# A Restormer-style block on one core: which bands put a chunk of the convolution on TensorE, where the first image's attention keeps its sums, and a new order

## The chip, the cores and the metric

The kernel runs on one core of a Trainium2 chip. The metric is the device time of one execution in microseconds; a kernel is run several times and the median is compared.

## The reference

The input x is 16 images of 128 channels and 96 × 96 pixels, all in float32. For each image the block computes, in this order:

```python
xn = layernorm(x, over channels)                  # norm 1
q, k, v = xn @ wq.T, xn @ wk.T, xn @ wv.T         # 8 heads of 16 channels
q, k = l2norm over the pixels of q, k
attn = softmax(q @ k.T / sqrt(16))                # 16 x 16 per head, a sum over all 9216 pixels
x = x + (attn @ v) @ wp.T
xn = layernorm(x, over channels)                  # norm 2
h1 = conv1x1(xn, w_in)                            # 128 -> 512 channels
h2 = depthwise_conv3x3(h1, w_dw)
x = x + conv1x1(gelu(h2), w_out)                  # 512 -> 128 channels
```

The attention is over channels, so an image needs its whole norm 1 before the attention, and the attention before its norm 2.

## The kernel before

Channels lie on the 128 partitions and pixels along the free dimension. An image is cut into 8 **bands** of 12 rows (1152 pixels) and 24 **units** of 4 rows (384 pixels); 16 images make 128 bands, numbered g = 0 to 127. The 512 hidden channels are 4 **chunks** of 128.

**Norms** (`norm`, lines 475 to 632). Norm 1 is called a, norm 2 is called b. Four tiles of 128 pixels make a batch q, 18 in an image. TensorE transposes them so that pixels lie on partitions (`forth`, L533), DVE takes the statistics (`stats`, L539) and the variance (L546), GpSimd raises it to the power of −1/2 (`power`, L550), DVE makes the shift (`shift`, L554), and ScalarE writes the normalized tiles zT (`scaled`, L573; for the first image, which uses h banks for its transposes, DVE does half of them, L563). For norm 1 TensorE then adds the tiles' products with themselves into one 128 × 129 sum in PSUM (`gram`, L583). It transposes them back (`back`, L609), and ScalarE puts them into the padded image xn (`place`, L613 and L615). Norm 2 starts from x plus the attention's result (`x2`: `mix`, L491, and either `residual` on DVE, L497, or `mixed` on ScalarE with a DMA that adds x, L500 and L503).

**Attention** (`attention`, lines 634 to 759) works on the gram alone. It is a chain of small steps that alternate between TensorE, DVE, GpSimd and ScalarE. Its first step (L660) copies the gram to SBUF; the later ones use other columns of the gram's own PSUM bank for their results. The planner has one such bank, `g`.

**Feed forward.** A chunk of a band is made in one of two ways. In a DVE job (`conv_job`), TensorE makes the hidden rows (`hidden`, L783), ScalarE copies them to SBUF (`kept`, L788) and makes three of the nine products (`product`, L799), two of which are added by accumulating DMAs that GpSimd issues (`add_products`, L807); DVE adds the six other taps (`tap`, L803), and ScalarE applies the gelu (`gelu`, L811). In the very last job there are no such DMAs: DVE adds all eight taps, and the gelu goes unit by unit. Or, for chunk 3 only (`PE_CHUNK`), TensorE does the 1 × 1 and the 3 × 3 convolution as nine matmuls per unit with weights made beforehand (`by_matmuls`, L853), and ScalarE applies the gelu (L859). `by_pe` (L898) says for which bands. At the end `ffn_out` multiplies the four chunks with w_out per unit (L876), DVE adds the result to x (L883), and SyncE issues the store (L887). The order of the four products is

```python
order = sorted(range(NCH), key=lambda n: (n != PE_CHUNK, n))
```

which is chunk 3 first, then 0, 1, 2.

**The order of the work** is made by a planner (`Plan`, lines 46 to 196). Each step is given an engine, a time that it is expected to take, what it reads and writes, and a place: a number of jobs, to which the table `AT` adds an offset by the kind of step. The planner runs the steps through a small event simulation: when an engine is free, it takes the step with the lowest place of those whose inputs are there and for which a buffer is free. The order that comes out is the order in which each engine executes; semaphores keep the dependencies on the chip. The planner also counts the buffers: 4 PSUM banks `h` (shared by the products of mix, hidden, conv and out, by the first image's transposes and by the weights' transposes), 2 banks `tr`, 1 bank `g`, 3 buffers zT, 9 buffers h3, 4 buffers pr, 2 and 5 buffers x1 and xb for bands of x. A TensorE matmul in float32 shows as two records in the profile.

Of the kernel before, what the change touches and what calls it, by code (L numbers as in the profile page):

```python
# [18 lines left out]
BR = 12  # L19
# [2 lines left out]
PE_OF = 7  # L22
TINY = 1e-20
DMA_TAPS = (1, 2)
QT = 4
H_BANKS = 4
X1_BUFS, XB_BUFS, PR_BUFS, H3_BUFS, ZT_BUFS = 2, 5, 4, 9, 3
IN_TURN = ("tr", "h3", "pr", "xb", "x1")
AT = dict(
    weights=0.9, zeros=6.55, load_a=-14.05, forth_a=-8.8, stats_a=-11.5, variance_a=-13.4, power_a=3.35,  # L30
    shift_a=-4.85, scaled_a=-0.8, gram=-2.9, back_a=-19.8, place_a=-18.9, attention=-9.75, mix=-10.05,
    residual=-13.2, mixed=-4.5, add_x=4.65, forth_b=-6.15, stats_b=1.25, variance_b=-4, power_b=-19,
    shift_b=-16.6, scaled_b=0.85, back_b=-14.75, place_b=-1.75, halo=1.55, hidden=-0, kept=-5.25,
    product=-4.6, products=2.35, add_last=-9.55, tap=6, add_first=25.15, gelu=-2.6, conv=1.9,
    conv_gelu=-2.9, out=2.85, add=5.05, store=1.6,
)
STEP = dict(hidden=0.1, products=0.5, tap=0.166, conv=1.6, conv_tap=0.03, out=0.8, out_part=0.05)
SLACK = 300
NORM1_END = 6.0
EARLY = 5  # L40
WAIT = dict(POOL=350, SP=1300, ACT=1300)
T_ADD, T_MOVE = 3100, 1800


class Plan:
# [44 lines left out]
    def order(self):  # L90
# [38 lines left out]
        def dispatch(engine, time):  # L129
            queue = queues[engine]  # L130
            while queue:
                item = heapq.heappop(queue)
                k = item[1]
                lacks = room(k)
                if lacks is None:
                    break
                waiting.setdefault(lacks, []).append(k)
            else:
                return
            o = ops[k]  # L140
            starts[k] = time
            idle[engine] = False
            for t in o[5]:
                self.slot[t] = free[t[0]].pop(0)
                if t[0] in IN_TURN:
                    turn[t[0]].pop()
                    wake(t[0], time)
            ns, result, own = o[1], o[6], o[7]
            if o[8]:
                self.dma = max(time + ns + WAIT[engine], self.dma) + o[8]  # L150
                result = own = self.dma + result - time
            elif engine == "POOL":
                rest = self.two - time
                ns, result = (ns, result) if rest <= 0 else (rest + 705, rest + result)
                own = result
            if o[9]:
                self.two = time + ns + 35
            push(time + own, "own", k)
            push(time + ns, "idle", k)
            push(time + result, "done", k)  # L160
# [39 lines left out]
def tile_restormer_block(  # L200
# [32 lines left out]
    NTOK = H * W  # L233
    HP, WP = H + 2, W + 1
    D = C // HEADS
    assert PE_CHUNK == NCH - 1 and BR * W >= 8 * P and QT % 2 == 0 and NU * TPU % QT == 0 and C == P and UT % P == 0 and H % BR == 0 and NCH == 4

    xv = x.rearrange("b c h w -> b c (h w)")
    ov = out.rearrange("b c h w -> b c (h w)")
# [16 lines left out]
    make_block_diagonal(nc, blocks, D)  # L256
    ones = const.tile([P, 1], F32, name="ones")
    nc.gpsimd.memset(ones, 1.0)
    mhalf = const.tile([P, QT], F32, name="mhalf")
    nc.gpsimd.memset(mhalf, -0.5)  # L260

    def column(v, name):
# [212 lines left out]
    def norm(i, second, place_of):  # L475
# [38 lines left out]
                xb = [xtok(b * UPB + k) for k in range(UPB)]  # L514
                add(at("add_x", s), add_x, [], xb)

        def pixels(s, q):

            d = {}
            tiles = range(q * QT, (q + 1) * QT)  # L520
            early = i == 0 and (not second or q < EARLY)
            key_ = "h" if early else "tr"
            by_dve = QT // 2 if early else 0

            def forth():
                if early:
                    d["pT"] = bank((name, q)).rearrange("p (t c) -> p t c", c=P)
                else:
                    d["pT"] = p_tr.tile([P, QT, P], F32, tag="tr", name=f"pT_{name}_{q}")
                for t in tiles:  # L530
                    b, j = divmod(t, TPB)
                    xt = (xbs if x_key(i, b, second) == "xb" else x1s)[i, b]
                    nc.tensor.transpose(d["pT"][:, t - tiles[0], :], xt[:, j * P : (j + 1) * P], ident)  # L533

            def stats(j):

                if j == 0:
                    d["st"] = small.tile([P, QT // 2, 6], F32, tag="st", name=f"st_{name}_{q}")
                nc.vector.bn_stats(  # L539
                    d["st"][:, j, :], d["pT"][:, 2 * j : 2 * j + 2, :].rearrange("p t c -> p c t")  # L540
                )

            def variance():
                d["mv"] = d["st"].rearrange("p j (t v) -> p (j t) v", v=3)
                ve = d["ve"] = small.tile([P, QT], F32, tag="ve", name=f"ve_{name}_{q}")
                nc.vector.tensor_scalar(ve, d["mv"][:, :, 2], 1.0 / C, EPS, ALU.mult, ALU.add)  # L546

            def power():
                rstd = d["rstd"] = small.tile([P, QT], F32, tag="rstd", name=f"rstd_{name}_{q}")
                nc.gpsimd.tensor_tensor(rstd, d["ve"], mhalf, ALU.pow)  # L550

            def shift():
                nb = d["nb"] = small.tile([P, QT], F32, tag="nb", name=f"nb_{name}_{q}")
                nc.vector.scalar_tensor_tensor(nb, d["mv"][:, :, 1], -1.0, d["rstd"], ALU.mult, ALU.mult)  # L554
                if by_dve:
                    take_zT()

            def take_zT():
                zTs[q] = zT_bufs[plan.slot["zT", (name, q)]]

            def also_scaled():
                for j in range(by_dve):
                    nc.vector.tensor_scalar(  # L563
                        zTs[q][:, j, :P], d["pT"][:, j, :], d["mv"][:, j, 1:2], d["rstd"][:, j : j + 1],
                        ALU.subtract, ALU.mult,
                    )

            def scaled():
                if not by_dve:
                    take_zT()  # L570
                zT = zTs[q]
                for j in range(by_dve, QT):
                    nc.scalar.activation(  # L573
                        zT[:, j, :P], d["pT"][:, j, :], AF.Identity,
                        bias=d["nb"][:, j : j + 1], scale=d["rstd"][:, j : j + 1],
                    )

            def gram():
                if q == 0:
                    grams[i] = p_g.tile([P, 4 * P], F32, tag="g", name=f"g_{i}")  # L580
                for t in tiles:
                    zt = zTs[q][:, t - tiles[0], :]
                    nc.tensor.matmul(  # L583
                        grams[i][:, : P + 1], lhsT=zt[:, :P], rhs=zt, start=(t == 0), stop=(t == NU * TPU - 1)
                    )

            tr, bt, zt = (key_, (name, q)), ("batch", (name, q)), ("zT", (name, q))
            units = {t // TPU: None for t in tiles}
            pe(110 * QT, at("forth" + ab, s), forth, [xtok(u) for u in units], [tr])
            for j in range(QT // 2):  # L590
                dve(341, at("stats" + ab, s), lambda j=j: stats(j), [tr], [bt])
            dve(80, at("variance" + ab, s), variance, [], [bt])
            op("POOL", 848, at("power" + ab, s), power, [], [bt], 881 + SLACK)
            dve(80, at("shift" + ab, s), shift, [], [bt, (*zt, 2)] if by_dve else [bt])
            if by_dve:
                dve(by_dve * 240, at("scaled" + ab, s), also_scaled, [tr, bt], [(*zt, 0)])
            act((QT - by_dve) * 343, at("scaled" + ab, s), scaled, [tr, bt], [(*zt, 1)])
            if not second:
                pe(QT * 220, at("gram", s), gram, [(*zt, 0), (*zt, 1), ("w", "ones")], [("g", i)])

        def channels(s, u):

# [22 lines left out]
            for u in range(NU):  # L625
                x2(place_of(u * TPU), u)
        u = 0
        for q in range(NU * TPU // QT):
            pixels(place_of(q * QT), q)
            while u < NU and (u + 1) * TPU <= (q + 1) * QT:  # L630
                channels(place_of(u * TPU), u)
                u += 1

    def attention(s, i):
# [2 lines left out]
        places_of = dict(srow="ma", kq="ma", em="ma", y="ma", gs="mb", e="mb", a="mb", mT="mb")  # L637
        columns = dict(ps_s=128, ps_u=256, ps_r=0, ps_n=128, ps_kq=256, ps_qk=384, ps_y=0, ps_m=128, ps_d=256)
        v = {}

        def sb(shape, tag, pool=att):
            v[tag] = pool.tile(shape, F32, tag=places_of.get(tag, tag), name=f"{tag}_{i}")
# [2 lines left out]
        def ps(shape, tag):  # L645

            c = columns[tag]
            v[tag] = grams[i][: shape[0], c : c + shape[1]]
            return v[tag]

        def step(engine, ns, also=()):
            def add(f):
                op(engine, ns, s, f, [("w", "qk")], [("g", i), ("m", i), *also], ns + 200 + SLACK)
            return add

        wide = [("x1", ("attention", i))]

        @step("DVE", 210)
        def _():
            nc.vector.tensor_copy(sb([P, P + 1], "gs"), grams[i][:, : P + 1])  # L660
            v["gsb"], v["s"] = v["gs"][:, :P], v["gs"][:, P:]
# [43 lines left out]
        def _():  # L705
            nc.vector.tensor_scalar(sb([P, 2], "n2"), v["ps_n"], 1e-24, None, ALU.max)

        @step("POOL", 848)
        def _():
            nc.gpsimd.tensor_tensor(sb([P, 2], "rn"), v["n2"], mhalf[:, :2], ALU.pow)  # L710

# [184 lines left out]
            move(at("store", p), lambda: store(0, UPB), [("xb", (i, b), k) for k in range(UPB)], [], T_MOVE)  # L896

    def by_pe(g):  # L898
        return g % PE_OF in PE_BANDS

    NG = B * NB
    jobs, first = [], []
# [56 lines left out]
```

## Time and profile before

| | |
|---|---|
| median of 8 runs | 4418.47 us (4414.09 to 4421.56) |
| profiled execution, its own time | 4422.32 us |
| its span | 4420.6 us |
| TensorE (PE) busy | 4309.6 us |
| VectorE (DVE) busy | 4272.2 us |
| ScalarE (ACT) busy | 4060.2 us |
| GpSimd (POOL) busy | 1881.5 us |
| taps on DVE, L803 | 2636 of 1408 ns, 3655.3 us |
| matmuls of the conv, L853 | 3942 records of 486 ns |
| matmuls of the output, L876 | 3072 records of 492 ns |

In the lines of the profile, PE is TensorE and PEld its loading of weights, DVE is VectorE, ACT is ScalarE, POOL is GpSimd and SP is SyncE. A timeline line gives the start and the length in microseconds, the engine, the source line, the operation, what is written and read (`h<-h,dw,h`), the shape and the count of merged instructions; the brackets give the idle time of the engine before it and what ended that. A line of waits gives who waited for whom, the sum in microseconds, the number of times and the longest. A line of a stretch gives the stretch, its length, then for each engine the busy time and the number of instructions, the granted TensorE clock, the share of the DMA engines and GB/s. The time of a matmul is modelled, so records overlap and the mean of one is longer than the distance from one to the next.

### The profile page before, as it was taken

How to read it: one execution, taken by the hardware profiler on the slowest of the kernel's cores; microseconds unless marked ns; L12 is line 12 of the kernel's file. 1: busy time of each engine (PE TensorE's matmuls, PEld its weight loads, DVE VectorE, ACT ScalarE, POOL GpSimd, SP SyncE). 2: the span in 40 equal slices, each digit the busy share in tenths (PEclk: the TensorE clock that was granted, in tenths of full speed). 3: DMA queues.
4: the chain of work that ended last, by engine and by line, in shares of the span. 5: the costliest groups of instructions: out<-in, count | busy, mean ns of one | idle time of the engine just before them, and what ended most of it. 6: DMA issues, size and time to landing. Idle time of an engine off the chain costs nothing. (4 is left out here: it accounts for less than half of the span.)

```text
span 4420.6 us, 53360 instructions
## 1 busy us (share of the span) xinstructions
PE 4309.6 (97%) x17782; PEld 2752.1 (62%) x17782; DVE 4272.2 (97%) x5681; ACT 4060.2 (92%) x7071; POOL 1881.5 (43%) x1620
## 2 busy tenths in 40 slices
PE   7999999999999999999999999999999999999997
PEld 6656666666666666666666666666666666666554
DVE  5999999999999999999999999999999999999998
ACT  4999999999999999999999999999999999989885
POOL 3444444344444444444444444444445444444331
PEclk9999999999999999999999999999999999999998
DMA  2778788787888878788887887878888888878886
GB/s 78 161 162 174 169 174 179 166 182 161 182 172 168 183 163 178 168 172 179 168 176 167 180 174 162 182 167 178 173 170 179 168 178 170 169 169 162 171 169 134
DMA packets 183635, 744.52 MB, mean 168 GB/s; under 512 B 21312, under 2 KB 22720, under 8 KB 183360
## 3 DMA queue, kind: packets, MB, share of 16 engines
q0 software_dynamic: 143856, 589.30, 70.5%
q1 hardware_dynamic: 37152, 151.01, 9.3%
q8 instruction: 140, 2.29, 0.2%
q10 hardware_dynamic: 2352, 0.81, 0.1%
q14 instruction: 135, 1.11, 0.1%
HBM read 148.85 MB, written 75.50 MB: 51 GB/s over the span
## 5 line engine op out<-in xcount | busy, mean ns | idle before, releaser
L803 DVE SCALAR_TENSOR_TENSOR h<-h,dw,h 128x1152 f32<-128x1152 f32 x2636 | 3655.3, 1408 | 5.8 <-ACT h L799 1.5
L853 PE MATMUL h<-xn,comp 128*128 128x384 f32 x3942 | 1421.1, 486 | 8.6 <-ACT x L500 5.0
L799 ACT ACTIVATE pr<-h,dw 128x1152 f32<-128x1152 f32 x876 | 1131.9, 1302 | 26.5 <-DMA pr<-pr 25.8
L876 PE MATMUL h<-h,woutT 128*128 128x384 f32 x3072 | 1115.4, 492 | 41.7 <-ACT h L788 17.6
L783 PE MATMUL h<-xn,winT 128*128 128x384 f32 (+1 forms) x2634 | 1034.2, 500 | 6.1 <-ACT h L859 2.4
L853 PEld LDWEIGHTS h<-xn,comp 128*128 128x128 f32 x3942 | 718.8, 189 | 465.3 <-issue 16.1
L876 PEld LDWEIGHTS h<-h,woutT 128*128 128x128 f32 x3072 | 562.2, 191 | 400.9 <-ACT h L788 28.3
L807 POOL DMA_DIRECT2D h<-pr x438 | 406.5, 928 | 846.5 <-issue 139.4
L788 ACT COPY h<-h 128x384 f32<-128x384 f32 (+1 forms) x1317 | 654.9, 532 | 93.7 <-PE h L783 70.6
L807 POOL DMA_DIRECT2D pr<-pr x438 | 403.2, 921 | 747.8 <-ACT pr L799 590.1
L550 POOL TENSOR_TENSOR rstd_b<-ve_b,mhalf 128x4 f32<-128x4 f32 x288 | 521.6, 1812 | 384.9 <-DVE ve_b L546 358.7
L550 POOL TENSOR_TENSOR rstd_a<-ve_a,mhalf 128x4 f32<-128x4 f32 x288 | 509.9, 1775 | 390.9 <-DVE ve_a L546 378.5
L783 PEld LDWEIGHTS h<-xn,winT 128*128 128x128 f32 x2634 | 474.6, 190 | 305.2 <-issue 35.1
L811 ACT ACTIVATE h<-h 128x1152 f32<-128x1152 f32 x441 | 529.3, 1201 | 70.4 <-DMA h<-pr 67.5
L799 ACT ACTIVATE h<-h,dw 128x1152 f32<-128x1152 f32 x439 | 569.8, 1298 | 5.0 <-PE h L876 1.2
L573 ACT ACTIVATE zT<-pT_b,nb_b,rstd_b 128x128 f32<-128x128 f32 x1132 | 438.4, 509 | 14.6 <-DVE nb_b L554 13.2
L573 ACT ACTIVATE zT<-pT_a,nb_a,rstd_a 128x128 f32<-128x128 f32 x1080 | 417.4, 508 | 20.5 <-DVE nb_a L554 17.5
L583 PEld LDWEIGHTS g<-zT 128*128 128x128 f32 x2304 | 292.1, 191 | 40.1 <-issue 2.1
L583 PE MATMUL g<-zT 128*128 128x129 f32 x2304 | 305.6, 275 | 0.2 <-DVE zT L563 0.2
L491 PE MATMUL h<-xn,mwT 128*128 128x384 f32 x768 | 286.0, 489 | 3.0 <-ACT h L788 1.4
L613 ACT ACTIVATE xn<-pB_b,b 128x384 f32<-128x384 f32 x384 | 243.3, 634 | 22.8 <-PE pB_b L609 21.7
L539 DVE BATCH_NORM_STATS2 st_b<-pT_b 128x6 f32<-128x256 f32 x566 | 237.6, 422 | 5.6 <-PE pT_b L533 5.4
(111 smaller groups left out, 3246.8 us busy)
## 6 DMA issues: line engine op xcount, KB each, us to landing
pr<-pr POOLq DMA_DIRECT2D x438, 576.0 KB, 5.4
h<-pr POOLq DMA_DIRECT2D x438, 576.0 KB, 6.2
x<-in_x_dram SPq DMA_DIRECT2D x128, 576.0 KB, 5.5
out_dram<-x SPq DMA_DIRECT2D x127, 576.0 KB, 3.7
x<-in_x_dram POOLq DMA_DIRECT2D x123, 576.0 KB, 7.0
out_dram<-x SPq DMA_DIRECT2D x3, 192.0 KB, 1.8
weights<-in_L_conv_w_in_dram ACTq DMA_DIRECT2D x1, 256.0 KB, 10.0
weights<-in_L_conv_w_out_dram ACTq DMA_DIRECT2D x1, 256.0 KB, 10.2
```

Source lines behind the costliest of these rows:

```text
L491: nc.tensor.matmul(rows(pm), lhsT=mats[i][0], rhs=interior(i, u), start=True, stop=True)
L550: nc.gpsimd.tensor_tensor(rstd, d["ve"], mhalf, ALU.pow)
L573: nc.scalar.activation(zT[:, j, :P], d["pT"][:, j, :], AF.Identity, bias=d["nb"][:, j : j + 1], scale=d["rstd"][:, j : j + 1],)
L583: nc.tensor.matmul(grams[i][:, : P + 1], lhsT=zt[:, :P], rhs=zt, start=(t == 0), stop=(t == NU * TPU - 1))
L783: nc.tensor.matmul(rows(ph), lhsT=winT[:, n, :], rhs=window(xn, r0 + r, e - r, 1), start=True, stop=True)
L788: nc.scalar.copy(window(h1_, r, e - r, 1), rows(d.pop(("ph", r))))
L799: nc.scalar.activation(to, shifted(t), AF.Copy, scale=dw[:, n, t : t + 1])
L803: nc.vector.scalar_tensor_tensor(h3, shifted(t), dw[:, n, t : t + 1], h3, ALU.mult, ALU.add)
L807: nc.gpsimd.dma_start(out=to, in_=d["pr", t], accum_op=ALU.add)
L811: nc.scalar.activation(h3, h3, AF.Gelu)
L853: nc.tensor.matmul(d["pc"], lhsT=comp[:, t, :], rhs=window(xn, r0 + dy, UR, dx), start=(t == 0), stop=(t == 8),)
L876: nc.tensor.matmul(rows(d["po"]), lhsT=woutT[:, n, :], rhs=h3s[g, n][:, s * UR : (s + 1) * UR, :], start=(k == 0), stop=(k == NCH - 1),)
```

## The change

Four things are edited.

1. `by_pe` counts bands from the last one: band g has its chunk 3 on TensorE where (127 − g) mod 7 is 0, 2, 4 or 6; before it was where g mod 7 is.
2. The attention of the first image uses a bank of the h set for all its steps but the first; the g bank is then free when the gram has been copied. The other images keep using g.
3. The planner's costs: the power on GpSimd counts 1000 ns instead of 848, the attention's own 700 instead of 848; the wait for a running tap is counted by another formula.
4. Most offsets in `AT` are new, so the order of the work is new.

Besides, the norm's code can now take several batches (`QB`) at once; with QB = 1 it issues the same instructions as before. The step that picks the zT buffer is now the one that writes it.

```diff
-QT = 4
+QT, QB = 4, 1
 AT = dict(
-    weights=0.9, zeros=6.55, load_a=-14.05, forth_a=-8.8, stats_a=-11.5, variance_a=-13.4, power_a=3.35,
-    shift_a=-4.85, scaled_a=-0.8, gram=-2.9, back_a=-19.8, place_a=-18.9, attention=-9.75, mix=-10.05,
-    residual=-13.2, mixed=-4.5, add_x=4.65, forth_b=-6.15, stats_b=1.25, variance_b=-4, power_b=-19,
-    shift_b=-16.6, scaled_b=0.85, back_b=-14.75, place_b=-1.75, halo=1.55, hidden=-0, kept=-5.25,
-    product=-4.6, products=2.35, add_last=-9.55, tap=6, add_first=25.15, gelu=-2.6, conv=1.9,
-    conv_gelu=-2.9, out=2.85, add=5.05, store=1.6,
+    weights=3.15, zeros=4.9, load_a=-14.3, forth_a=-7.1, stats_a=-4.2, variance_a=-11.35, power_a=1.4,
+    shift_a=-1.25, scaled_a=1.3, gram=-2.35, back_a=-17.7, place_a=-22.25, attention=-9.3, mix=-9.85,
+    residual=-9.65, mixed=-5, add_x=10.2, forth_b=-5.55, stats_b=0.75, variance_b=-2.55, power_b=-21.7,
+    shift_b=-15.55, scaled_b=2.55, back_b=-16.75, place_b=-2.05, halo=-2.15, hidden=-0.05, kept=-5.35,
+    product=-6.7, products=3.65, add_last=-5.65, tap=4.9, add_first=21.35, gelu=-7.9, conv=1.85,
+    conv_gelu=-4.85, out=3, add=4.45, store=1.65,
 )
+T_POWER = 1000
...
             elif engine == "POOL":
                 rest = self.two - time
-                ns, result = (ns, result) if rest <= 0 else (rest + 705, rest + result)
+                ns, result = (ns, result) if rest <= 0 else (rest + ns - 143, rest + result - 143)
                 own = result
...
-            op("POOL", 848, at("power" + ab, s), power, [], [bt], 881 + SLACK)
+            op("POOL", T_POWER, at("power" + ab, s), power, [], [bt], T_POWER + 33 + SLACK)
-            dve(80, at("shift" + ab, s), shift, [], [bt, (*zt, 2)] if by_dve else [bt])
+            dve(80, at("shift" + ab, s), shift, [], [bt])
...
+        apart = i == 0
+        mine = [("h", ("attention", i)) if apart else ("g", i), ("m", i)]
...
             c = columns[tag]
-            v[tag] = grams[i][: shape[0], c : c + shape[1]]
+            v[tag] = (bank(("attention", i)) if apart else grams[i])[: shape[0], c : c + shape[1]]
...
-                op(engine, ns, s, f, [("w", "qk")], [("g", i), ("m", i), *also], ns + 200 + SLACK)
+                op(engine, ns, s, f, [("w", "qk")], [*mine, *also], ns + 200 + SLACK)
...
-        @step("DVE", 210)
+        @step("DVE", 210, [("g", i)])
         def _():
             nc.vector.tensor_copy(sb([P, P + 1], "gs"), grams[i][:, : P + 1])
...
-        @step("POOL", 848)
+        @step("POOL", 700)
         def _():
             nc.gpsimd.tensor_tensor(sb([P, 2], "rn"), v["n2"], mhalf[:, :2], ALU.pow)
...
     def by_pe(g):
-        return g % PE_OF in PE_BANDS
+        return (NG - 1 - g) % PE_OF in PE_BANDS
```

## The prediction

> **What bounds the kernel now.** I read the page's busy rows first, then the waits of DVE, then the busy times by stretch at both ends, then the timeline there.
>
> ```profile
> PE 4309.6 (97%) x17782; PEld 2752.1 (62%) x17782; DVE 4272.2 (97%) x5681; ACT 4060.2 (92%) x7071; POOL 1881.5 (43%) x1620
> ```
>
> DVE is busy for 4272.2 of 4420.6 us, so 148.4 us idle are all there is to win on it while its work stays. PE is as full, but its busy time covers pipelined instructions with gaps between them. I take DVE as the bound wherever it has work, and PE where DVE has to wait for its first work. DVE's idle time lies in three places. By stretch (PE, PEld, DVE, ACT, POOL, then clock, DMA share, GB/s), the head after image 0's norm 1, then the tail:
>
> ```profile
> 60.50:81.70 21.20, 14.28 (x61) 10.07 (x62) 6.40 (x25) 7.87 (x21) 2.68 (x3) 0.65 0.19 56
> 81.70:95.00 13.30, 13.02 (x86) 10.60 (x85) 9.99 (x32) 6.44 (x16) 6.01 (x6) 0.92 0.29 89
> 95.00:109.00 14.00, 13.62 (x70) 9.11 (x70) 10.61 (x32) 10.90 (x25) 4.00 (x4) 1.00 0.01 1
> 109.00:130.00 21.00, 20.68 (x82) 12.60 (x81) 20.14 (x23) 20.94 (x35) 5.86 (x5) 1.00 0.53 114
> ```
>
> ```profile
> 4360.00:4390.00 30.00, 29.65 (x91) 16.84 (x89) 30.00 (x27) 21.40 (x27) 6.02 (x7) 1.00 0.78 161
> 4390.00:4405.70 15.70, 0.00 (x0) 0.00 (x0) 15.52 (x12) 2.33 (x2) 0.86 (x1) 0.65 0.48 113
> 4405.70:4421.00 15.30, 10.75 (x24) 5.85 (x24) 1.68 (x4) 1.35 (x3) 0.00 (x0) 0.80 0.10 39
> ```
>
> From 60.5 to 81.7 the first image's attention runs as a chain of small steps, and every engine is half idle. From 81.7 to 109 PE is full (26.64 of 27.30 us) while DVE is not (20.60): DVE waits for PE to bring the first band. From 109 on DVE is full. In the last 31 us the order turns round: PE does nothing for 15.7 us while DVE is full, then PE works alone for 10.75 us. The timeline of the two ends:
>
> ```profile
> 61.24 0.29 DVE L660 COPY gs<-g 128x129 f32<-128x129 f32 x1 [0.83 <-PE g L583]
> 80.38 0.16 DVE L758 COPY d<-g 128x1 f32<-128x1 f32 x1 [0.68 <-PE g L754]
> ...
> 86.10 1.06 PE L583 MATMUL g<-zT 128*128 128x129 f32 x8
> ```
>
> ```profile
> 4402.48 1.16 ACT L811 ACTIVATE h<-h 128x1152 f32<-128x1152 f32 x1 [7.75 <-DMA h<-pr]
> 4405.74 1.35 ACT L811 ACTIVATE h<-h 128x384 f32<-128x384 f32 x3 [2.10 <-DVE h L803]
> 4406.32 10.75 PE L876 MATMUL h<-h,woutT 128*128 128x384 f32 x24 [16.67 <-ACT h L811]
> 4411.84 0.56 DVE L883 TENSOR_TENSOR x<-h,x 128x384 f32<-128x384 f32 x1 [6.13 <-PE h L876]
> ...
> 4414.52 0.56 DVE L883 TENSOR_TENSOR x<-h,x 128x384 f32<-128x384 f32 x1 [2.12 <-PE h L876]
> 4417.11 0.56 DVE L883 TENSOR_TENSOR x<-h,x 128x384 f32<-128x384 f32 x1 [2.02 <-PE h L876]
> ```
>
> The bank g is read at 61.24 by attention's first step and held to 80.38 by its later ones; the next image's grams come at 86.10. At the end all 24 records of the last band's output product (3 units, 4 chunks, two records each) wait for one gelu. `ffn_out` explains it: its order begins with chunk 3, and in band 127 chunk 3 is not made on TensorE but by the last DVE job. The rest of DVE's idle time, in the middle, is mostly one wait:
>
> ```profile
> DVE nb_b L554 <- POOL rstd_b L550: 30.0, 31, 1.6
> DVE nb_a L554 <- POOL rstd_a L550: 26.0, 31, 0.9
> DVE x L883 <- PE h L876: 16.1, 15, 6.1
> ```
>
> That is 56.0 us in 62 of 576 shifts, 0.90 us each.
>
> **The counting of bands.** There are 128 bands and 128 mod 7 is 2, so before, bands 7k, 7k+2, 7k+4, 7k+6 have chunk 3 on TensorE; counted from the end these are bands 127, 125, 123, 121, 120 and so on. Written forwards, each pair (7k, 7k+1) swaps its kinds, and nothing else. Both have 73 such bands and 439 DVE jobs, so the total work of PE, DVE, ACT and DMA is unchanged. Seventeen inner swaps shift work by one band and back; I cost them at nothing, since in the middle both kinds are in flight together (nine h3 buffers).
>
> The last pair counts. Let T be the end of the last tap (4405.7 before). Before, the last add ends at 4417.67, T + 11.95: gelu 0.5, 24 records 10.75, one add 0.56, small gaps. After, chunk 3 of the last band comes from TensorE early, so 6 records per chunk go out as chunks 3, 0 and 1 finish, and only the 6 of the last job (chunk 2) must follow T. The price depends on the clock. The first 8 of the 24 records took 5.5 us (4406.32 to 4411.84), 0.69 each; the next 8 took 2.7 (to 4414.52), 0.33 each. Chunk 1's gelu should end as its counterpart now does, at 4403.64 (T − 2.1), after some idle time of PE. Slow to begin with, its 6 records take 4.1 us, to T + 2.1; the first two of the last six are still slow (1.4), the other four fast (1.3), to T + 4.8; gap and add 0.6: T + 5.4. That saves 6.5 us. Were PE fast throughout, chunk 1 would be done by T and the last six records would follow the gelus as they come: T + 0.6 + 2.0 + 0.6 = T + 3.2, a saving of 8.8. Were only chunk 3 out in time, 18 records would follow T, 5.5 + 10 × 0.33 = 8.8 instead of 10.75: 2.0. I take 6.5, because PE's granted clock stood at 0.65 over the 15.7 us before T, with PE idle; its new work there is 5 us in pieces.
>
> The Trainium skill, "TensorE: Matmul & The Clock Gate", Part 1, says that the array halves its clock after about 3.4 us idle and recovers after about 3.4 us of sustained work. That speaks against the full saving, as the rows do, but its slow stretch is 2 us shorter than the 5.5 us seen here; by it, as an estimate, the saving would be about 7.5 us. No number here uses it.
>
> What covers the moved work: the 27 products of the last band's conv (54 records at 0.33 us, 18 us) must be done before T. PE is full from 4330 to 4390, but band 126 gives up just as much there, and the 15.7 us of idle PE lie behind it.
>
> In the first pair, band 0 loses its 54 records (19.2 us on PE between 109 and 150) and gains a fourth DVE job. They begin at 110.98, after the first tap at 108.86, so they do not hold that tap. PE is full from 109 to 150 and so is ACT (20.94 of 21 us, to 130); DVE loses only 1.8 us there. I cost it at nothing, with 2 us either way.
>
> **Attention of image 0 in a bank of h.** The chain keeps its instructions and durations. It now holds an h bank from the first step to the last, a queue shared by mix, hidden, conv and out. Nothing else uses h in that time: the last weights transposes are at 59, the first mix at 81.73. If later weights (their place moves from 0.9 to 3.15) fell into it, three banks remain. What is freed is g, at 61.5 instead of 80.5. Of the five batches of grams between 81.7 and 95 (5.12 us of PE), two have zT ready by 66 and two more follow the landing of image 1's second band at about 73; the fifth comes too late. Four batches are 4.1 us off a stretch where PE is full and DVE waits. PE also stays warmer: that stretch ran at 0.92, and 8% of 13.3 us is 1.0. So the first tap comes up to 5.1 us sooner, and since DVE is the bound afterwards, the end too. It could be nothing, if the new order spends the freed time on image 1's transposes and places. I take 4.5, with 0 to 7.
>
> **New costs and order.** T_POWER only changes what the planner believes. With a tap running when the power is dispatched, the expected result moves from rest + 1181 to rest + 1190 ns, which is nothing; without one, from 1181 to 1333. Taps fill 3655 of DVE's 4272 us, so the second case is one in seven, and 152 ns moves a shift past a 1.4 us tap in one case of nine: 56 × 1/7 × 1/9, about 1 us. The power also counts 152 ns longer on POOL, which is 43% busy. The new places reorder all queues: PE, DVE, ACT, POOL's powers against its DMA issues (L807, L503), and SP's loads and stores. Stats of norm 1 lose rank (−11.5 to −4.2) but still outrank every tap. No row prices a new order; its bounds come from the 56 us, halved (28 less) or grown by half (28 more). I take 1 less, since the rules of rank against taps stay as they are.
>
> **Sum.** 6.5 + 4.5 + 1 = 12 us. The profiled execution took 4422.3 us, so 4410.3; its median companion runs are 3.8 lower (4418.47), so 4406.5.
>
> **The rivals.** (1) The new order also halves DVE's wait for POOL: 28 more, less the 1 counted, 4379. For: that wait is the largest idle time left on DVE. Against: the planner's model of it is nearly the same. (2) The gains are given back: head 0, tail 2 to 5, 4414 to 4417. For: PE and ACT are full right behind the first tap. (3) Slower: powers queue on POOL behind accumulating DMAs that wait for ACT (POOL waits 590 us on products of L799), shifts stall, and DVE, the bound, stalls with them. The price is 0.90 us for a late shift; 13 more of 576 eat up the 12 us, 23 more make it slower by 0.2%. At 50 more, 4451; at 35, 4438. (4) The bands are the only thing that acts, the freed bank being filled by nothing: 4411, inside the forecast's range.
>
> **How the numbers follow.** Forecast with rival 4: 0.50, own range 4396 to 4418. Rival 1: 0.20. Rival 2: 0.12. Rival 3: 0.18. A measurement of this kernel can tell about 0.2%, 8.8 us, from no change. Of the forecast I put 0.44 beyond that; with rival 1, faster is 0.64. Same: 0.06 and 0.11 of rival 2, 0.17. Slower: 0.18 and 0.01. The range reaches from rival 1 to the mild end of rival 3, 4374 to 4432.
>
> **What would show it.** In the profile after: PE records of L876 before the last tap's end, only about 6 to 12 behind it, and the last add at most 6 us after T; L583 records for image 1 before attention's last copy; the first tap near 104; 62 late shifts, give or take 10. It is wrong if the first tap is not earlier, if 18 or more records still follow T, or if DVE's idle time between the first and last taps (90 us now) has changed by more than the two ends together.

## The result, and the profile after

The kernel after takes 4404.79 us (median of 10 runs, 4402.22 to 4408.36); the kernel before, run beside it, 4419.09. The ratio is 0.9969, with a 95% interval of 0.9961 to 0.9977, which is 13.7 us less. The prediction was 4406.5, in a range of 4374 to 4432. The profiled executions are 17.8 us apart (4422.32 and 4404.52); the split below is of their spans.

The busy row of the page after:

```profile
PE 4307.5 (98%) x17782; PEld 2754.0 (63%) x17782; DVE 4268.5 (97%) x5681; ACT 4057.3 (92%) x7071; POOL 1866.6 (42%) x1620
```

The numbers of instructions are those of before: the work is the same, and its order differs. To see where the time went, both spans are cut at the first and at the last tap on DVE. These are the busy times by stretch (PE, PEld, DVE, ACT, POOL, then clock, DMA share, GB/s), first of the kernel before:

```profile
0.00:108.86 108.86, 82.86 (x518) 67.08 (x519) 64.31 (x228) 48.95 (x118) 35.64 (x62) 0.92 0.24 79
108.86:4405.71 4296.85, 4215.95 (x17241) 2679.14 (x17239) 4206.27 (x5450) 4009.90 (x6951) 1845.85 (x1558) 1.00 0.82 171
4405.71:4420.62 14.91, 10.75 (x24) 5.85 (x24) 1.67 (x4) 1.35 (x3) 0.00 (x0) 0.79 0.11 40
```

and of the kernel after:

```profile
0.00:107.66 107.66, 83.30 (x523) 66.96 (x524) 63.25 (x225) 48.60 (x119) 34.51 (x61) 0.95 0.25 80
107.66:4394.63 4286.97, 4220.31 (x17254) 2685.43 (x17252) 4203.56 (x5454) 4007.36 (x6951) 1832.13 (x1559) 1.00 0.82 172
4394.63:4402.81 8.18, 3.90 (x6) 1.65 (x6) 1.67 (x3) 1.35 (x3) 0.00 (x0) 0.76 0.19 72
```

The head is shorter by 1.2 us, the middle by 9.9 and the end by 6.7. DVE's idle time (a stretch less its busy time) shows more: 44.6 and 44.4 us in the head, so nothing was won there; 90.6 and 83.4 in the middle; 13.2 and 6.5 at the end. The other 3.8 us are DVE's busy time, which differs for the same instructions: 4272.2 and 4268.5 us.

The end, in the timeline after:

```profile
4382.18 11.10 PE L882 MATMUL h<-h,woutT 128*128 128x384 f32 x28 [3.80 <-DVE x L889]
...
4391.76 2.87 DVE L809 SCALAR_TENSOR_TENSOR h<-h,dw,h 128x1152 f32<-128x1152 f32 x2
...
4394.66 1.35 ACT L817 ACTIVATE h<-h 128x384 f32<-128x384 f32 x3 [4.66 <-DVE h L809]
4395.24 3.90 PE L882 MATMUL h<-h,woutT 128*128 128x384 f32 x6 [1.97 <-ACT h L817]
...
4399.17 0.56 DVE L889 TENSOR_TENSOR x<-h,x 128x384 f32<-128x384 f32 x1 [0.66 <-PE h L882]
```

Six records wait for the last gelu, where 24 did; 18 of the last band's 24 were done before (the last 18 of the 28 that end at 4393.28; the last tap ends at 4394.63).

DVE's waits between the taps (who for whom, us, times, longest; window 111 to 4385), first before and then after:

```profile
DVE nb_b L554 <- POOL rstd_b L550: 30.0, 31, 1.6
DVE nb_a L554 <- POOL rstd_a L550: 24.4, 27, 0.9
DVE x L883 <- PE h L876: 5.8, 12, 0.9
```

```profile
DVE nb_b L556 <- POOL rstd_b L552: 29.5, 32, 1.2
DVE nb_a L556 <- POOL rstd_a L552: 18.8, 20, 2.3
```

The wait for POOL fell from 54.4 us in 58 shifts to 48.3 us in 52. That is 6 of the 7 us; the smaller waits moved by 1 to 3 us in both directions.

### The profile page after: what moved, and what is told of

It is laid out like the page before. It is cut to its first block, busy times and chain, and to the rows that moved or that the text cites. A ratio compares the mean times of both kernels' runs of the same rounds, so it can differ in the third digit from the quotient of the medians.

```text
span 4402.8 us, 53391 instructions
## 1 busy us (share of the span) xinstructions
PE 4307.5 (98%) x17782; PEld 2754.0 (63%) x17782; DVE 4268.5 (97%) x5681; ACT 4057.3 (92%) x7071; POOL 1866.6 (42%) x1620
## 4 chain that ended last, share of the span: by engine, by line
PE 34%; DVE 13%; ACT 3%; DMA 3%; issue 1%; POOL 1%; POOLq 0%; DVEq 0%; ACTq 0%
DVE h L809 11%; PE h L859 10%; PE h L882 9%; PE h L789 7%; DMA h<-pr 2%; PE h L492 2%; PE g L583 2%; PE pB_b L613 1%; PE pT_b L534 1%; PE pB_a L613 1%; PE pT_a L534 1%; DVE x L889 1%; ACT zT L573 1%; ACT pr L805 1%; DVE st_b L541 1%
## 5 line engine op out<-in xcount | busy, mean ns | idle before, releaser
L859 PE MATMUL h<-xn,comp 128*128 128x384 f32 x3942 | 1401.7, 486 | 5.9 <-DVE x L889 2.5
L789 PE MATMUL h<-xn,winT 128*128 128x384 f32 (+1 forms) x2634 | 1049.7, 501 | 7.4 <-ACT h L865 3.6
L882 PEld LDWEIGHTS h<-h,woutT 128*128 128x128 f32 x3072 | 560.7, 191 | 391.1 <-issue 44.6
L552 POOL TENSOR_TENSOR rstd_a<-ve_a,mhalf 128x4 f32<-128x4 f32 x288 | 494.4, 1719 | 354.7 <-DVE ve_a L548 330.5
L573 ACT ACTIVATE zT<-pT_b,nb_b,rstd_b 128x128 f32<-128x128 f32 x1132 | 437.3, 505 | 14.2 <-DVE nb_b L556 13.7
```

Of the source, the lines that this page charges most:

```text
L573: nc.scalar.activation(zT(q)[:, k, :P], d["pT", q][:, k, :], AF.Identity, bias=d["nb"][:, t : t + 1], scale=d["rstd"][:, t : t + 1],)
L789: nc.tensor.matmul(rows(ph), lhsT=winT[:, n, :], rhs=window(xn, r0 + r, e - r, 1), start=True, stop=True)
L859: nc.tensor.matmul(d["pc"], lhsT=comp[:, t, :], rhs=window(xn, r0 + dy, UR, dx), start=(t == 0), stop=(t == 8),)
L882: nc.tensor.matmul(rows(d["po"]), lhsT=woutT[:, n, :], rhs=h3s[g, n][:, s * UR : (s + 1) * UR, :], start=(k == 0), stop=(k == NCH - 1),)
```

## The experiments

Each kernel was compared with the kernel before, run on the same chip; the ratio has its 95% interval. The kernel before took 4419 to 4423 us on the chips used, so kernels from different chips are compared by their ratios. The parts of the change come first, each in a kernel of its own.

**Bands counted from the last, alone.**

```diff
-        return g % PE_OF in PE_BANDS
+        return (NG - 1 - g) % PE_OF in PE_BANDS
```

> The kernel before with one edit: bands counted from the last one; old places, old costs, attention of image 0 in g. The theory that the end is worth 6 to 7 us by itself: the time behind the last tap falls from 14.9 us to about 8.2, with 6 records of the output product behind it; the time falls by 6 to 7 us, give or take what the middle gains or loses by the planner's order shifting (3 us either way). The rival that the saving at the end needs the new places: more than 6 records remain behind the last tap, and the time stays within 3 us of before.

Measured: 4437.66 us, ratio 1.0039 (1.0026 to 1.0051): slower by 17 us. Both halves of the expectation must be told apart. The stretches of its middle and end:

```profile
110.32:4433.78 4323.46, 4236.14 (x17259) 2692.06 (x17257) 4210.31 (x5450) 4013.44 (x6951) 1837.51 (x1558) 0.99 0.82 170
4433.78:4441.55 7.77, 3.62 (x6) 1.50 (x6) 1.67 (x4) 1.35 (x3) 0.00 (x0) 0.78 0.20 76
```

and its largest wait of the middle for PE (window 111 to 4433):

```profile
DVE x L883 <- PE h L876: 22.2, 35, 2.0
```

The end does what was said: 7.8 us instead of 14.9, with six records. But the middle is 26.6 us longer. DVE idles 113.1 us there, 22.6 more than before, and the largest part of that is not the wait for POOL (53 us, where there were 54) but output adds that wait for PE (22 us where there were 6). A theory for the end alone could not say that, and the time that was expected, 6 to 7 us less, was missed.

**Attention in an h bank, alone.** The edit is that of the change: `mine`, `ps` and the first step.

> The kernel before with one edit: the first image's attention in a bank of h. By the prediction the first tap comes 4.5 us sooner and the time falls by 4.5 us. The theory now: two batches of grams go into attention's time, but the stretch behind it is filled again by image 1's transposes; the first tap moves by less than 2 us and the time by less than 3 us either way.

Measured: 4420.49 us, ratio 0.9999 (0.9990 to 1.0008): nothing. The grams of image 1 and the first mix in its timeline:

```profile
65.45 1.95 PE L583 MATMUL g<-zT 128*128 128x129 f32 x16
...
82.22 1.93 PE L583 MATMUL g<-zT 128*128 128x129 f32 x8
83.94 1.43 PE L491 MATMUL h<-xn,mwT 128*128 128x384 f32 x2
```

16 records of grams went into attention's time and 8 more between its end (the copy of d at 80.87) and the first mix, which came at 83.94 instead of 81.73. From the first mix to the first hidden product it took 21.8 us, where it took 22.0 before, although 16 fewer records of grams lay in it. So the first tap came at 110.35 instead of 108.86. In the two traces the order of the instructions on every engine is the same from about 0.31 ms on, so this kernel tests the bank and is not a new order as a whole.

**New places and costs, alone** (the kernel after with the old `by_pe` and attention in g; the small edit of the step that picks the zT buffer stays in it).

```diff
-        apart = i == 0
+        apart = False
...
-        return (NG - 1 - g) % PE_OF in PE_BANDS
+        return g % PE_OF in PE_BANDS
```

> The kernel after without its two structural edits: bands counted from the first, image 0's attention in g; new places and costs alone. By the prediction 1 us less than before. The theory now, from the two profiles: DVE's idle time between first and last tap falls from 90.6 us to about 83 and DVE's busy time by 3 to 4 us, so 8 to 11 us less; 24 records remain behind the last tap. The rival that these come from the edits of structure and not from the places: less than 3 us.

Measured: 4403.90 us, ratio 0.9961 (0.9948 to 0.9973). That is 17 us less, where 8 to 11 were expected. The places and costs alone give as much as the whole change; the intervals overlap. Its stretches:

```profile
105.52:4389.22 4283.70, 4216.39 (x17254) 2681.50 (x17252) 4206.90 (x5454) 4010.66 (x6955) 1847.19 (x1559) 1.00 0.82 172
4389.22:4404.40 15.18, 10.94 (x24) 5.87 (x24) 1.67 (x4) 1.35 (x3) 0.00 (x0) 0.78 0.10 39
```

The end is the long one, 15.2 us. The gain is ahead of it: the first tap comes 3.3 us sooner, and DVE idles 76.8 us in the middle instead of 90.6. DVE's waits there (window 111 to 4385):

```profile
DVE nb_b L556 <- POOL rstd_b L552: 25.7, 27, 1.4
DVE nb_a L556 <- POOL rstd_a L552: 12.6, 14, 2.1
```

That is 41 late shifts for 58 and 38.3 us for 54.4: the prediction's first rival, at about half its size. DVE's busy time did not fall with it, so that part of the expectation was wrong. New places with the old costs were not run.

**The order of the last band's output product, alone.** The bands are those of before.

```diff
-        order = sorted(range(NCH), key=lambda n: (n != PE_CHUNK, n))
+        order = sorted(range(NCH), key=lambda n: (n != PE_CHUNK or g == NG - 1, n))
```

> The kernel before with one edit in ffn_out: in band 127 alone the output product takes the chunks in the order 0, 1, 2, 3. The bands stay as they were, so this tests the step that chunk 3 in front of the queue is what holds all 24 records. If so: 6 records behind the last tap, the last add about 5.4 us behind it instead of 11.95, and 6 to 7 us less in time. If the records are held by something else (PE's banks, the bands' work), 12 or more remain and the time falls by less than 3 us.

Measured: 4412.96 us, ratio 0.9982 (0.9973 to 0.9991), 8 us less. The timeline of its end:

```profile
4393.42 3.90 PE L876 MATMUL h<-h,woutT 128*128 128x384 f32 x6 [3.21 <-ACT h L811]
...
4402.32 6.59 PE L876 MATMUL h<-h,woutT 128*128 128x384 f32 x12 [5.00 <-ACT h L811]
4404.36 1.35 ACT L811 ACTIVATE h<-h 128x384 f32<-128x384 f32 x3 [2.10 <-DVE h L803]
4407.66 1.85 DVE L883 TENSOR_TENSOR x<-h,x 128x384 f32<-128x384 f32 x3 [3.33 <-PE h L876]
```

The products go out as the chunks are done, and 8.15 us lie behind the last tap, with ten records in them; six were expected. The last add ends 5.2 us behind the last tap. The middle has 89.3 us of idle DVE, as before. In the trace every engine has the instructions of before in the order of before, and that is why the gain can be read from the time itself: the end gives 6.8 of the 8.1 us between the two profiles. Chunk 3 at the head of PE's queue was what held all 24 records.

**The planner's new costs, alone** (power 1000, attention's 700, the formula; old places).

> The kernel before with only the planner's costs of the change: power 1000 ns, attention's power 700, the new formula for a running tap; old places, bands and bank. The prediction gave this 1 us less, since the expected end of a power is nearly the same. The theory that the new costs are what makes shifts late less often: DVE's wait for POOL between the taps falls from 54 us to about 40 and the time by 10 to 15 us. The rival that the new places do it: the wait stays within 5 us of 54, the time within 4 us.

Measured: 4432.85 us, ratio 1.0019 (1.0010 to 1.0028), slower. Its wait for POOL in the middle is 60 us (65 times). The costs do not make shifts late less often by themselves, and the time moved by more than the rival's 4 us too.

**A change without meaning.** Each of four kernels moves one place by 0.05, the smallest step in the table: two start from the kernel before, two from the kernel after. The first:

```diff
-    product=-4.6, products=2.35, add_last=-9.55, tap=6, add_first=25.15, gelu=-2.6, conv=1.9,
+    product=-4.6, products=2.35, add_last=-9.55, tap=6.05, add_first=25.15, gelu=-2.6, conv=1.9,
```

> The kernel before with one place moved by the smallest step of the table (tap 6 to 6.05), which has no meaning of its own. It measures how far the time moves with the order alone. If the order's details matter little: within 2 us of before, DVE's idle time between first and last tap within 3 us of 90.6. If any other order scatters by 5 us or more, the 16 us by which the bands alone made it slower, and the part of the new places, are partly draws of that scatter.

> The kernel before with another place moved by the smallest step (out 2.85 to 2.9). The first such nudge cost 18 us. By the theory of single good draws 10 to 25 us slower than before, though a draw near it or better is possible; if it is within 2 us of before, the first nudge was the exception.

> The kernel after with one place moved by the smallest step of the table (tap 4.9 to 4.95). Theory: both tables are single good draws, fitted to the structure they stand in, and a neighbour loses 10 to 20 us, all of it between the first and the last tap; so 4412 to 4425 and DVE's idle time there 90 to 105 us instead of 83. The rival that the new places are better as a whole: within 4 us of the kernel after, about 4405 to 4409.

> The kernel after with another place moved by the smallest step (out 3 to 3.05). A second draw of the same: by the theory of single good draws 4412 to 4425, by the rival 4405 to 4409. The part behind the last tap stays near 8.2 us in both.

| | edit | median us | ratio to before (95%) | DVE idle, middle | end |
|---|---|---|---|---|---|
| before | | 4419 to 4423 | 1 | 90.6 | 14.9 |
| | tap 6 to 6.05 | 4441.74 | 1.0045 (1.0033 to 1.0058) | 100.5 | 15.0 |
| | out 2.85 to 2.9 | 4434.76 | 1.0032 (1.0021 to 1.0043) | 97.8 | 14.6 |
| after | | 4404.79 | 0.9969 (0.9961 to 0.9977) | 83.4 | 8.2 |
| | tap 4.9 to 4.95 | 4417.90 | 0.9994 (0.9985 to 1.0003) | 90.1 | 9.1 |
| | out 3 to 3.05 | 4416.75 | 0.9986 (0.9977 to 0.9995) | 91.8 | 6.4 |

All four are slower than the kernel they start from, by 7 to 20 us. So the first expectation's "details matter little" fell, and the theory that both tables are single good draws (orders that happen to be good, whose neighbours are worse) held for these four: the order that comes out of the planner scatters by more than most of what was to be explained. The traces bear this out. The orders of these kernels leave those of their starting points 0.15 to 0.3 ms after the start, and the time between first and last tap grows by 11 to 17 us. In the two kernels above that keep the order of before (the bank, from 0.31 ms on, and the order of the products), that time is within 0.6 us of before. What does not fit is the second half of the theory, that a table is fitted to the structure that it stands in: the new places with the old structure have the least idle time of all, 76.8 us. The rival held in part as well: the neighbours of the new table stand some 20 us below those of the old one (mean ratio 0.9990 against 1.0039), of which the end accounts for 7. The end of the last kernel, 6.4 us where 8.2 was expected, had a faster clock (see the last section). Two neighbours each are too few to say more of the rest.

The waits of DVE in the middle of the first nudged kernel (window 111 to 4385):

```profile
DVE nb_b L554 <- POOL rstd_b L550: 31.4, 34, 1.6
DVE nb_a L554 <- POOL rstd_a L550: 22.9, 25, 1.6
DVE x L883 <- PE h L876: 10.5, 22, 1.2
DVE st_a L539 <- PE pT_a L533: 7.5, 16, 1.1
```

The wait for POOL is 54.3 us, as before. What grew is many small waits for PE (adds 5.8 to 10.5, statistics of norm 1 3.0 to 7.5), and DVE's busy time by 6.8 us. A worse order is not worse in one place.

**The kernel after with attention back in g.**

> The kernel after with the first image's attention back in g. By the prediction 4.5 us slower than the kernel after. The theory now: the bank is worth under 2 us, so 4403 to 4407, with the first tap within 2 us of 107.7; the order shifts again and may add 3 us either way.

Measured: 4415.47 us, ratio 0.9981 (0.9972 to 0.9989). By the ratios that is about 5 us slower than the kernel after, with intervals that overlap; the kernel before took 4423.28 beside this one and 4419.09 beside the kernel after. If it is slower, then not by the bank's mechanism: the first tap comes earlier without the bank, at 105.39 instead of 107.66, and the loss lies in the middle (DVE idle 90.3). It is no farther off than the nudged neighbours, so it cannot be told from one more draw.

**Image 1's norm 1 later**, to test whether PE's other work holds the first band:

```diff
-        start1 = job_of(NB * (i - 1)) if i else end1 - 8
+        start1 = job_of(NB * (i - 1)) + (4 if i == 1 else 0) if i else end1 - 8
```

> The kernel after with image 1's norm 1 planned to begin four jobs later, so that little of it lies between the first attention and the first tap. If PE's work for image 1 is what holds the first band, as the prediction had it, the time from the first mix to the first hidden product (20.5 us after) falls to 12 to 15 us and the first tap comes to about 100 instead of 107.7. If the chain of small steps of image 0's own norm 2 holds it, it stays above 18 us. The time as a whole is moved by the other order too and is not read for this.

Measured: between the first mix and the first hidden product lie 18.8 us (20.5 in the kernel after), although only 8 records of grams (32), 6 of back (15) and 4 of forth (8) of image 1 are left in it. The stretches of this time, rounded to tenths, of the kernel after and then of this one:

```profile
79.70:100.10 20.40, 19.66 (x116) 14.73 (x116) 15.35 (x46) 9.53 (x24) 5.98 (x6) 0.97 0.10 30
```

```profile
77.10:95.90 18.80, 16.34 (x80) 11.13 (x81) 13.84 (x40) 6.49 (x15) 5.01 (x5) 0.91 0.00 0
```

PE lost 36 of 116 records and stands idle for 2.5 us, but the way shortened by 1.7 us only. Part of that is the clock. The two lines are the same mixes, of the kernel after and then of this one, and the third is a stretch of this one:

```profile
92.60 0.91 PE L492 MATMUL h<-xn,mwT 128*128 128x384 f32 x2 [0.16 <-ACT zT L573]
```

```profile
87.03 1.65 PE L492 MATMUL h<-xn,mwT 128*128 128x384 f32 x2 [0.40 <-ACT zT L573]
```

```profile
88.00:90.00 2.00, 2.00 (x7) 1.29 (x6) 0.62 (x1) 0.73 (x2) 0.00 (x0) 0.50 0.00 0
```

With less to do, PE stood idle for 1.8 us at 82.8 and for shorter times behind it, and from about 87 to 90 its granted clock was 0.50. From the start of these mixes to the record behind the next seven it took 3.84 us, where it took 2.52, so the slow clock cost about 1.3 us, as an estimate. The kernel after has a slow piece too: its first four mixes took 2.0 us at a clock of 0.70, where four later ones took 1.4. With both taken off, the way would be some 17.5 us in place of 19.9: shorter by 2.4 us, and between the two expectations. The chain that ended last runs through this stretch: 12.0 of its 18.7 us are PE, but only 1.6 of these are work for image 1. So it is image 0's own mixes and norm 2, whose steps wait for each other, that hold the first band. The first tap came at 101.95, 5.7 us sooner: 2.6 by an earlier first mix, 1.7 by this way and 1.5 by a shorter way from hidden product to tap. The whole kernel took 4416.04, ratio 0.9985 (0.9976 to 0.9994), so a first tap that is 5.7 us sooner did not make it faster than the kernel after. Its order differs from that of the kernel after up to about 2.4 ms.

**New places, bands as before, the last band's output in order of readiness.** The two gains that can be told apart, together.

> New places and costs, with the bands counted from the first, attention in g, and in band 127 alone the output product in the order of chunks 0, 1, 2, 3. If the two gains add up: 4404 less 6 to 8.5, so 4395 to 4398, faster than the kernel after by 7 to 10 us, with 6 records to 12 behind the last tap.

Measured: 4398.34 us, ratio 0.9946 (0.9932 to 0.9959). It beats both kernels; from the kernel after it differs by 0.0023, about 10 us, and from the new places alone by 0.0015, about 7 us, as expected, though the last two intervals overlap. Only its times are read, so how many records follow its last tap is not known.

## Why the prediction was right, and where it was not

The sum was right, 12 us for 13.7, but only one of its three terms was: the bank's 4.5 us did not come, and the order, counted with 1, gave about as much instead. That the two errors cancel is luck. Of the signs that the prediction named, the six records behind the last tap, the grams ahead of attention's last copy (16 records) and the count of late shifts (59 for 62, over the whole span) came true, and the first tap near 104 did not. DVE's idle time between the taps changed by 7.2 us, just less than the two ends together (7.9), which was one of its signs of being wrong.

**The end** (6.5 us): right in mechanism and size. The last add ends 5.1 us behind the last tap (4399.73 less 4394.63), foreseen as 5.4; the shorter stretch is worth 6.7 us. Two kernels show it apart from the rest, by the bands and by the order of the products. The path was a little different, and two differences cancelled: chunk 1's gelu ended 4.6 us ahead of the last tap and not 2.1, so its products were out 1.4 us ahead of that tap, but all of the last six were slow (0.65 us each), where two were to be.

**The freed bank** (4.5 us): wrong; alone it gave nothing. Two steps failed. First, of the four batches of grams that were to move into attention's time, two did. The band of the other two had landed at 71.0, sooner than foreseen, but their zT were written from 76.5 to 79.4, behind transposes, statistics, powers and shifts between attention's own steps, and attention ended at 78.5. Second, and more: the prediction took the batches "off a stretch where PE is full and DVE waits" and let the first tap gain what PE is spared. PE was busy for 26.64 of 27.30 us, but with the work of image 1 that filled its gaps. With most of that work gone, the way to the first hidden product was 1.7 us shorter (about 2.4 without the slow clock in both). The first tap came at 107.66.

**The new order** (1 us): wrong by the most. The places and costs by themselves gave 17 us, and in the kernel after the middle is 9.9 us shorter. The step that failed was to price an order without rows by the rules of rank, which had hardly changed. The first rival, which put it at up to 28 us by way of the late shifts, was nearer the cause in the kernel with places and costs alone (16 us less wait for POOL), but in the kernel after that wait fell by 6 only.

**The bands** away from the end (0): not shown to be nothing. Alone they lengthened the middle by 26.6 us in the profile (about 24 by the median) and won 7 at the end; moving one place by 0.05 lengthened it by 11 to 17, so all or part of it can be the order's scatter. I leave it open. For the same reason the parts do not add up: bands +17, bank 0, places −17, all together −13.7.

The third rival (powers that queue on POOL make it slower) did not come, and the slow neighbours are not slow by it: in the first nudged kernel the wait for POOL is what it was. Why a neighbouring order loses 7 to 20 us is known here only as a sum of small waits; which early step sets them off was not found.

## What to carry to other kernels

Where a greedy planner makes the order, an edit can change the whole order, and its time is then one draw: move a place by the smallest step a few times before and after, and compare the sets, or judge the edit by the stretch that it acts on. Where the trace shows that the order elsewhere is unchanged, the time itself can be read. A mechanism at the end of a kernel can be priced from its timeline, and an order in which the operand that comes last stands first in an engine's order is cheap to find and to mend. A full engine ahead of a waiting one is not yet the bound: see whether its work belongs to the chain that is waited for.

## What the runs showed of the hardware

Six records of the last output product took 3.90 us in the kernel after, where the granted clock behind the last tap was 0.76, and 2.20 us in its second nudged neighbour, where it was 0.99. Both come behind 28 records without a gap (11.10 us after, 12.32 us in the neighbour) and an idle time of PE of nearly the same length (1.97 and 1.85 us), so a gap of 2 us ended in the slow clock in one of them and not in the other. I had not expected DVE's busy time to depend on the order: for the same 5681 instructions it was 4268.5 us in the kernel after and 4278.9 us in the first nudged kernel, one execution of each. In the kernels with the bank and with the order of the products alone, which keep the order of before, it was 4273.0 and 4272.9 us, for 4272.2 before. The cause was not looked for.
